# Halved background products, another DMA queue and centred projection weights in a fused attention and feed-forward kernel

## The chip, the cores and the metric

The kernel runs on one core of a Trainium2 chip. The core has a matrix engine (PE, TensorE, with its weight loads shown apart as PEld), three engines for elementwise work and reductions (DVE = VectorE, ACT = ScalarE, POOL = GpSimd), a synchronisation engine (SP) that mostly issues DMAs, and DMA queues that SP, ACT and POOL can each feed. Every engine works through its own instructions in order and waits for others through semaphores. The metric is the device time of one execution in microseconds (us), given as the median of several runs. A profile is a further execution, recorded by the hardware, with its own time.

## The reference

One transformer-like layer over a sequence of 4096 tokens with 256 features, all in float32: causal attention with 16 heads of 16 features, and a feed-forward part with four ternary weight matrices and 1024 hidden features. Cut to what matters:

```python
def _L0_attn_ref(x, w_attn, b_attn, w_proj, b_proj):
    q, k, v = jnp.split(x @ w_attn + b_attn, 3, axis=-1)      # then split in 16 heads
    logits = jnp.einsum('bhqd,bhkd->bhqk', q, k) * scale
    weights = jax.nn.softmax(jnp.where(causal, logits, -jnp.inf), axis=-1)
    out = jnp.einsum('bhqk,bhkd->bhqd', weights, v)
    return out @ w_proj + b_proj
...
x = x + _layernorm(_L0_attn_ref(_layernorm(x), ...))
x = x + _layernorm(_L0_ffn_ref(_layernorm(x), ...))
```

Two facts are used below: the layer norm of the attention's output follows the projection `w_proj` directly, and a layer norm subtracts the mean over the 256 features of each token.

## The kernel before

**Blocks and items.** The sequence is cut into NB = 8 blocks of QB = 512 tokens, block j being four tiles of 128 tokens (NT = 4). Attention works block by block over queries, and in a block over G = 4 groups of four heads: 32 items (j, g). An item goes over the key tiles kt = 0 to 4j + 3. `steps(j)` lists its steps: one for each key tile up to the first on the diagonal, and two that pack the three narrower diagonal tiles. A step has two units (`SharedUnit`, one in the last step), one for each pair of heads. So an item has 8j + 5 units, and attention 1056.

**A unit** is three pieces of work. `products()` (line 843) multiplies q and k on PE into a two-bank tile `s` of PSUM, 128 x 1024 scores. `maximum()` (line 852) reduces these to a running maximum on DVE. `finish()` (line 859) takes the exponential of the tile on ACT, with a per-block shift that was set from earlier maxima, and on diagonal tiles POOL zeroes the masked part with `affine_select` (line 866). There are three tiles `s`, so the scores of a unit wait for the exponential three units earlier. `Values.step` (line 930) multiplies the exponentials with v into `av`, some units later.

**Order.** Everything stands under a manual schedule: each engine executes in the order in which the Python code emits. The main loop emits a unit's scores, then perhaps a values step, then its maximum and exponential, and after each step calls `bg.even(...)`, which emits pieces of background work.

**Background work** is a queue of generators. `prep(j)` makes the features of block j: it loads and normalises x (mean and spread by two ACT passes, `mean_of` and `spread_of`, or by DVE for the first two blocks), transposes it on PE (`pt`, line 633), and multiplies it with the attention weights: `features` for k and q (`pk`, `pq`, line 525) and then `pv` for v (line 650). `features` copies the product to `full` (ACT, line 534), splits it in a rounded high part `hi` (line 542) and the rest `lo` (line 544), and stores each twice in DRAM (line 549), from where `queries` and `keys` load rows for the scores (line 557). In blocks 0 and 1 the split is on DVE and the `lo` stores are issued by POOL; later the split is on POOL and all stores are issued by SP. `full`, `hi`, `lo`, for k and for q, and the bank of the products are single buffers. `project(j)` loads the attention's output, scales it by the reciprocal sums on POOL, multiplies it with `w_proj` (`py`, line 314), copies it and adds the bias, takes the mean (`mean_of`, line 203) and the squared deviation (`spread_of`, line 211) of each tile on ACT, scales and shifts by them on POOL (line 224) and adds x. `halve_weights` rounds the feed-forward weights on POOL, four operations at a time (lines 1009 to 1012), one round in four steps.

A generator yields a mark before a piece: `PE`, `ACT` or True, and `HALF` between two pieces of one accumulation, which keeps the bank to that job. `even(every)` counts steps and emits one PE piece when the count is a multiple of `every`, and one ACT piece one step before that. `every` is 1 in blocks 0 and 1, 2 in blocks 2 and 3, and 3 later; from block 2 on, it isn't called on the diagonal steps. A PE piece is one matmul with 512 columns of a `pk` or `pq` (there are two to a product), or two matmuls with 256 columns for one tile of `pv` or `py`.

**The start.** `prep(0)` and `prep(1)` are run up to their transposes, then `biases()` folds the value bias through `w_proj` into `bp` (line 1106), then `prep(0)` is run to its end, with the loads of the first two items in between. `prep(1)` is left to the background.

**After attention** the feed-forward part runs over the eight blocks with split (high and low) activations on PE; the last projection, `project(7)`, runs there.

## Time and profile before

| | |
|---|---|
| median of 3 runs | 2053.86 us (2051.06 to 2056.44) |
| the profiled execution | 2048.42 us |
| its span, first to last instruction | 2046.5 us |
| mean granted PE clock | 0.986 |
| first maximum / last maximum of attention | 39.81 / 1374.4 us |
| granted clock from 39.8 to 92.8 us (block 0) | 0.77 |

Busy time in stretches that begin with the first maximum of a block, in us:

| stretch | length | units | PE | DVE | ACT | POOL |
|---|---|---|---|---|---|---|
| start | 39.8 | | 16.3 | 11.0 | 6.4 | 17.1 |
| block 0 | 53.0 | 20 | 39.9 | 29.0 | 30.0 | 17.0 |
| block 1 | 75.1 | 52 | 68.0 | 63.5 | 66.8 | 37.4 |
| block 2 | 107.0 | 84 | 97.4 | 99.7 | 102.1 | 53.9 |
| block 3 | 147.9 | 116 | 135.4 | 137.7 | 136.9 | 68.4 |
| block 4 | 185.7 | 148 | 161.6 | 173.5 | 174.1 | 79.4 |
| block 5 | 216.7 | 180 | 186.3 | 209.8 | 206.0 | 91.8 |
| block 6 | 253.8 | 212 | 218.7 | 246.2 | 240.9 | 95.0 |
| block 7 | 295.4 | 244 | 245.0 | 288.1 | 275.4 | 38.0 |
| feed-forward | 672.1 | | 656.8 | 351.4 | 160.7 | 54.2 |

A line of the groups reads: line of the code, engine, operation, tile written <- tiles read, shape written <- shape read, count | busy time, mean ns of one | idle time of the engine just before them, and what ended most of it. A line of the timeline reads: start, length (both in us), engine, line, operation, tiles, shapes, count of instructions merged, and in brackets the idle time before and what ended it. The length of merged instructions runs from the start of the first to the end of the last. Instructions of one engine overlap a little, so the time from start to start is shorter than the mean time of one.

### The profile page before, as it was taken

To read this page: it belongs to the slowest core of one execution; us is meant where nothing else is said; L and a number is where in the kernel's file an instruction comes from. 1 tells how busy PE (TensorE), PEld (TensorE's weight loads), DVE (VectorE), ACT (ScalarE), POOL (GpSimd) and SP (SyncE) were. 2 spreads that over 40 slices of the span, in tenths; PEclk is the share of its full clock that TensorE was granted. 3 is DMA by queue.
4 is the path that set the end of the run, shared out by engine and by line. 5 is a ranking of instruction groups with operands and counts; after the bars stand their busy time and mean duration, and the time that the engine had idled before them with its cause. 6 is when DMAs were issued, how large, how long until landed. Compare 5 with 4: busy or idle time off the path is not lost.

```text
span 2046.5 us, 28401 instructions
## 1 busy us (share of the span) xinstructions
PE 1825.3 (89%) x10518; PEld 932.5 (46%) x10518; DVE 1609.8 (79%) x1894; ACT 1399.2 (68%) x1598; POOL 552.2 (27%) x871
## 2 busy tenths in 40 slices
PE   4799989988888888888888887889999999999997
PEld 2333332322322322223222222228888888888886
DVE  3689998998999999999999999985546456465453
ACT  2699999999999999999999998982212222222221
POOL 3264545434435335333333110000120000000000
PEclk8899999999999999999999998999999999999999
DMA  6756645444235333553234213103100000000000
GB/s 168 229 179 219 191 133 180 147 154 159 98 131 183 116 103 124 161 163 115 76 136 156 98 44 101 63 9 114 53 11 21 15 7 21 1 21 21 1 11 15
DMA packets 134909, 202.09 MB, mean 99 GB/s; under 512 B 16064, under 2 KB 60736, under 8 KB 134752
## 3 DMA queue, kind: packets, MB, share of 16 engines
q1 hardware_dynamic: 130496, 194.56, 29.3%
q0 software_dynamic: 2480, 4.35, 1.0%
q8 instruction: 87, 1.43, 0.3%
q10 hardware_dynamic: 1776, 1.18, 0.3%
q14 instruction: 70, 0.57, 0.1%
HBM read 137.91 MB, written 62.13 MB: 98 GB/s over the span
## 4 chain that ended last, share of the span: by engine, by line
PE 46%; ACT 21%; DVE 19%; issue 6%; DMA 4%; POOL 2%; SPq 1%; ACTq 0%; POOLq 0%; DVEq 0%
PE z L1358 21%; ACT e_s L859 19%; DVE mx L852 18%; PE av L930 7%; PE s L843 7%; PE za L1358 3%; PE zb L1358 2%; PE pyf L1440 2%; DMA k<-k 1%; PE py L314 1%; PE pk L525 1%; PE pv L650 1%; PE pq L525 1%; ACT junk L211 1%; DMA q<-hiq 0%
## 5 line engine op out<-in xcount | busy, mean ns | idle before, releaser
L852 DVE TENSOR_REDUCE mx<-s 128x1 f32<-128x1024 f32 x1056 | 1219.8, 1217 | 72.1 <-PE s L843 66.6
L859 ACT ACTIVATE e_s<-s,shift 128x1024 f32<-128x1024 f32 x1056 | 1153.6, 1117 | 104.9 <-DVE mx L852 81.9
L843 PE MATMUL s<-q,k 64*128 64x512 f32 (+3 forms) x2304 | 517.7, 468 | 161.2 <-ACT e_s L859 144.7
L930 PE MATMUL av<-e_s,v 128*32 128x512 f32 (+2 forms) x4576 | 572.8, 575 | 7.9 <-POOL e_s L866 5.7
L843 PEld LDWEIGHTS s<-q,k 64*128 64x128 f32 x2304 | 208.9, 185 | 752.9 <-ACT e_s L859 652.2
L1425 ACT ACTIVATE fb<-z,sh 128x512 f32<-128x512 f32 x128 | 88.1, 689 | 364.8 <-PE z L1358 340.2
L1358 PE MATMUL z<-hb_0l,h 128*128 128x512 f32 x512 | 199.5, 390 | 0.0
L1358 PE MATMUL z<-hb_0h,h 128*128 128x512 f32 x512 | 199.5, 390 | 0.0
L866 POOL TENSOR_SCALAR_AFFINE_SELECT e_s<-e_s 128x256 f32<-128x256 f32 (+1 forms) x224 | 94.7, 440 | 337.4 <-ACT e_s L859 337.4
L233 POOL TENSOR_TENSOR rstd<-ve,neghalf 128x4 f32<-128x4 f32 (+1 forms) x22 | 20.8, 944 | 608.8 <-DVE ve L231 603.0
L930 PEld LDWEIGHTS av<-e_s,v 128*32 128x32 f32 x4576 | 97.2, 109 | 151.5 <-issue 116.1
L1325 DVE CAST hb_1h<-fb 128x512 fp32r<-128x512 f32 x64 | 27.4, 428 | 155.7 <-ACT fb L1425 155.7
L1402 ACT ACTIVATE sl<-za,s 128x512 f32<-128x512 f32 x64 | 44.0, 690 | 120.4 <-PE za L1358 60.9
L1325 DVE CAST hb_0h<-fb 128x512 fp32r<-128x512 f32 x64 | 28.1, 440 | 99.6 <-ACT fb L1425 99.6
L1358 PEld LDWEIGHTS z<-hb_0h,h 128*128 128x128 f32 x512 | 96.1, 188 | 20.0
L1358 PEld LDWEIGHTS z<-hb_0l,h 128*128 128x128 f32 x512 | 96.2, 188 | 19.8
L1011 POOL TENSOR_SCALAR wc<-wc 128x256 f32<-128x256 f32 x88 | 75.8, 861 | 7.8
L1010 POOL TENSOR_TENSOR wc<-wc,wh 128x256 f32<-128x256 f32 x88 | 64.3, 730 | 7.2
L1012 POOL TENSOR_TENSOR fit<-fit,wc 128x256 f32<-128x256 f32 x88 | 64.2, 730 | 7.3
L1009 POOL CAST wh<-wc 128x256 fp32r<-128x256 f32 x88 | 35.0, 397 | 108.4 <-DMA wc<-in_h_t_dram 75.9
L1440 PE MATMUL pyf<-w,hb_1l 128*128 128x256 f32 x256 | 61.8, 284 | 0.0
L1440 PE MATMUL pyf<-w,hb_1h 128*128 128x256 f32 x256 | 61.7, 283 | 0.0
(257 smaller groups left out, 1970.3 us busy)
## 6 DMA issues: line engine op xcount, KB each, us to landing
k<-k SPq DMA_DIRECT2D x288, 256.0 KB
q<-q SPq DMA_DIRECT2D x64, 256.0 KB
x<-in_x_dram SPq DMA_DIRECT2D x16, 512.0 KB
k<-hik SPq DMA_DIRECT2D x32, 256.0 KB
q<-hiq SPq DMA_DIRECT2D x32, 256.0 KB
wc<-in_h_t_dram SPq DMA_DIRECT2D x64, 128.0 KB
r_h<-wh SPq DMA_DIRECT2D x64, 128.0 KB
h<-r_h SPq DMA_DIRECT2D x32, 256.0 KB
```

The source lines that it names most:

```text
L843: nc.tensor.matmul(self.both[:, i, col : col + n], lhsT=kT[G * j + g, c, pr][r, tt * P : (tt + 1) * P], rhs=qT[j, g][pr][r, QB - n :], sta ...
L852: nc.vector.tensor_reduce(next(columns), self.both.rearrange("p a n -> p (a n)"), AX.X, ALU.max)
L859: nc.scalar.activation(e, self.both, AF.Exp, bias=shifts[j])
L866: nc.gpsimd.affine_select(out=here, in_=here, compare_op=ALU.is_ge, fill=0.0, base=0, pattern=[[0, here.shape[1]], [1, P]], channel_multip ...
L930: nc.tensor.matmul(self.av[h * HW : (h + 1) * HW, QB - n :], lhsT=vb[kt // NT][:, kt % NT, o : o + HW], rhs=of(es, h), start=(kt == 0 or k ...
L1010: nc.gpsimd.tensor_tensor(w, w, hi, ALU.subtract)
L1011: nc.gpsimd.tensor_scalar(w, w, 0.0, None, ALU.is_equal)
L1012: nc.gpsimd.tensor_tensor(fit, fit, w, ALU.mult)
L1325: nc.vector.tensor_copy(hi, full)
L1358: nc.tensor.matmul(ps, lhsT=w[c], rhs=single(part[:, c, :]), start=(c == 0 and i == 0), stop=(c == kc - 1 and i == parts - 1),)
L1425: nc.scalar.activation(h, z, AF.Gelu, scale=sc[:, oc : oc + 1])
L1440: nc.tensor.matmul(ps[:, 0:D], lhsT=single(part[:, c, t * P : (t + 1) * P]), rhs=(w3_r if halves else w3_sb)[:, c, :], start=(c == 0 and i ...
```

## The change

**Halves of pieces.** In the attention pass, `pk` and `pq` are computed for 256 of the 512 tokens at a time, each over both parts of the features, so that a product has four pieces (one matmul with 256 columns each) in place of two. `pv` and `py` give a piece for each matmul, and the four transposes of a bank are split in two and two.

**Rates.** `even(products, every, acts)` emits up to `products` PE pieces when the count of steps is a multiple of `every`, and an ACT piece once in `acts` steps. Blocks 0 and 1 get two PE pieces a step, blocks 2, 3, 4 and 7 one piece a step, blocks 5 and 6 one piece in two steps. ACT pieces come every 1, 1, 2, 2, 3, 4, 4, 2 steps. Block 2 now gets pieces on its diagonal steps too.

**Queue.** The low halves of block 0 are stored through ACT's queue in place of POOL's; those of block 1 stay on POOL's.

**Ahead of the first scores** `prep(1)` is run until its first k product is stored: two banks of transposes, the product `pk`, its split and the issue of its stores.

**Centred weights.** `biases()` subtracts from each row of `w_proj` its mean over the output features, and from `bp` its mean, so that the projection's output has mean zero over the features. `project` (for all blocks but the last) drops `mean_of` and the shift: `spread_of` takes the plain square, and POOL only scales.

**Order.** Before the first block's feed-forward norm is queued, in item (7, 2), `project(6)` is run to its end.

```diff
-    def even(self, every):
+    def even(self, products, every, acts):
...
         self.at += 1
-        pe, act = not self.at % every, not (self.at + 1) % every
+        pe = 0 if self.at % every else products
+        act = self.at % acts == 1 % acts
         for job in list(self.work):
             if job[3] in (self.PE, self.HALF):
-                if pe and self.open in (None, job):
-                    pe = False
+                while pe and job[3] in (self.PE, self.HALF) and self.open in (None, job):
+                    pe -= 1
                     self.run(job)
...
             for t in range(2):
-                yield room.within(t)
                 for c in range(DC):
+                    mark = room.within(DC * t + c, c > 0)
+                    if mark:
+                        yield mark
                     nc.tensor.matmul(
...
             for t in range(NT):
-                mean_of(y[:, t, :], mv, t)
-                yield Background.ACT
-                spread_of(y[:, t, :], mv, t)
+                spread_of(y[:, t, :], mv, t, 0.0)
                 yield Background.ACT if t < NT - 1 else True
...
+                nc.gpsimd.tensor_scalar(
+                    y[:, t, :], y[:, t, :], rstd[:, t : t + 1], None, ALU.mult
+                )
...
-                def within(self, n):
-                    return Background.HALF if shared and n else Background.BESIDE
+                def within(self, n, fine=False):
+                    if shared:
+                        return Background.HALF if n else Background.BESIDE
+                    return None if fine else Background.BESIDE
...
-                for d in range(DC):
-                    yield room.within(d)
+                cuts = 2 if shared else 1
+                for n, (cut, d) in enumerate(product(range(cuts), range(DC))):
+                    yield room.within(n)
+                    at = slice(cut * QB // cuts, (cut + 1) * QB // cuts)
                     nc.tensor.matmul(
-                        ps,
+                        ps[:, at],
                         lhsT=wqk[d][:, i * D + c * P : i * D + (c + 1) * P],
-                        rhs=xTs[j][:, d, :],
+                        rhs=xTs[j][:, d, at],
...
-                        queue = nc.gpsimd if shared and j < 2 and half else nc.sync
+                        queue = (nc.scalar, nc.gpsimd)[j] if shared and j < 2 and half else nc.sync
...
                     for t in range(NT):
+                        if shared and t == NT // 2:
+                            yield Background.HALF
                         nc.tensor.transpose(
...
             def biases():
                 nc.vector.tensor_scalar(bqk[:, 0:DC], bqk[:, 0:DC], SCALE, None, ALU.mult)
+                mean = stat.tile([P, DC], F32, tag="mean", name="mean")
+                nc.vector.tensor_reduce(mean, wp, AX.X, ALU.add)
+                nc.vector.tensor_scalar(mean, mean, -1.0 / D, None, ALU.mult)
+                for c in range(DC):
+                    nc.vector.tensor_scalar(
+                        wp[:, c, :], wp[:, c, :], mean[:, c : c + 1], None, ALU.add
+                    )
...
                 nc.vector.tensor_tensor(bp, bp, ps, ALU.add)
+                nc.vector.tensor_reduce(mean[:, 0:1], bp, AX.X, ALU.add)
+                nc.vector.tensor_scalar(mean[:, 0:1], mean[:, 0:1], -1.0 / D, None, ALU.mult)
+                nc.vector.tensor_scalar(bp, bp, mean[:, 0:1], None, ALU.add)
...
                 bg.work[0][3] = Background.PE
+                while ("k", 1, 0) not in stored:
+                    bg.step()
...
+                    bg.finish(("project", NB - 2))
                     bg.add(("norm", 0), norm_block(0, room, first_features), NORM)
...
-                    if j < 2 or p < NT * j:
-                        bg.even(1 + j // 2 - j // 6)
+                    if j < 3 or p < NT * j:
+                        bg.even(1 + (j < 2), 1 + (4 < j < NB - 1), (1, 1, 2, 2, 3, 4, 4, 2)[j])
```

More of the change, by code (lines that the diff above doesn't have):

```diff
@@ L2 @@
 from contextlib import ExitStack
-from itertools import chain, cycle
+from itertools import chain, cycle, product
 import concourse.bass as bass
@@ L205, in mean_of, with spread_of @@
         )
-    def spread_of(src, mv, t):
+    def spread_of(src, mv, t, shift=None):
         lent.append(True)
@@ L211, in spread_of @@
         nc.scalar.activation(
-            junk, src, AF.Square, bias=mv[:, t, 0:1], accum_out=mv[:, t, 1:2]
+            junk,
+            src,
+            AF.Square,
+            bias=mv[:, t, 0:1] if shift is None else shift,
+            accum_out=mv[:, t, 1:2],
         )
@@ L347, in project @@
         for t in range(NT):
-            (normalize if last else shift_and_scale)(
-                y[:, t, :], y[:, t, :], mv, rstd, t, nc.gpsimd
-            )
+            if last:
+                normalize(y[:, t, :], y[:, t, :], mv, rstd, t, nc.gpsimd)
+            else:
+                nc.gpsimd.tensor_scalar(
+                    y[:, t, :], y[:, t, :], rstd[:, t : t + 1], None, ALU.mult
+                )
             nc.gpsimd.tensor_tensor(y[:, t, :], y[:, t, :], xj[:, t, :], ALU.add)
@@ L647, in prep @@
                     for t in range(2):
-                        yield room.within(t)
                         for c in range(DC):
+                            mark = room.within(DC * t + c, c > 0)
+                            if mark:
+                                yield mark
                             nc.tensor.matmul(
@@ L1269, in feed_forward, with within @@
             class Room:
-                def within(self, n):
-                    return Background.BESIDE
+                def within(self, n, fine=False):
+                    return None if fine else Background.BESIDE
                 def bank(self, name):
```

## The prediction, made before the changed kernel was run

> **What bounds the kernel now.** I read the shares of busy time, the groups by line, stretches by block, then the timeline where the largest engine pauses.
>
> ```profile
> PE 1825.3 (89%) x10518; PEld 932.5 (46%) x10518; DVE 1609.8 (79%) x1894; ACT 1399.2 (68%) x1598; POOL 552.2 (27%) x871
> ...
> L852 DVE TENSOR_REDUCE mx<-s 128x1 f32<-128x1024 f32 x1056 | 1219.8, 1217 | 72.1 <-PE s L843 66.6
> L859 ACT ACTIVATE e_s<-s,shift 128x1024 f32<-128x1024 f32 x1056 | 1153.6, 1117 | 104.9 <-DVE mx L852 81.9
> ```
>
> Attention runs from the first maximum (39.81 us) to the last (1374.4), the feed-forward part from there to 2046.5. The second is the tensor engine's (656.8 busy of 672.1) and keeps its instructions, so it counts as unchanged. In attention, 1056 units pass through scores (PE), maximum (DVE), exponential (ACT), with three score tiles. Five maxima back to back take 5.75 us, one alone 1.23: the pace is (5.75 - 1.23)/4 = 1.13 us. 1056 x 1.13 = 1193 us of the stretch's 1334.6; the other 141 us are DVE's small work and its waits. ACT can do an exponential in 1.0 us (a small activation starts 1.0 after it), so it has about 12% to spare. What the waits are:
>
> ```profile
> 649.02 0.51 PE L843 MATMUL s<-q,k 64*128 64x512 f32 x2
> ...
> 649.46 1.13 PE L525 MATMUL pq<-xT,wqk 128*128 128x512 f32 x2
> ...
> 650.51 0.49 PE L843 MATMUL s<-q,k 64*128 64x512 f32 x2
> ...
> 650.94 1.07 PE L930 MATMUL av<-e_s,v 128*32 128x512 f32 x8
> 651.05 1.23 DVE L852 TENSOR_REDUCE mx<-s 128x1 f32<-128x1024 f32 x1 [0.19 <-PE s L843]
> ...
> 651.93 0.73 PE L843 MATMUL s<-q,k 64*128 64x512 f32 x4
> ...
> 652.47 1.22 DVE L852 TENSOR_REDUCE mx<-s 128x1 f32<-128x1024 f32 x1 [0.19 <-PE s L843]
> ```
>
> The background product `pq` occupies PE for 1.05 us (649.46 to the next scores at 650.51). The following scores are late, the maximum starts 0.28 us over the pace; the scores after it stand behind `av` and are again 0.29 late. One such product costs 0.57 us. In blocks 4 to 7 this pair returns every 7.36 us, where three steps of 2.26 us should take 6.79.
>
> **Products in halves of what they were.** The program order of the old kernel has 85 such products among the scores of blocks 2 to 7 (15, 19, 17, 14, 16, 4). In blocks 4 to 7: 51 x 0.57 = 29 us. In blocks 2 and 3 the rows show less, 0.3 to 0.65; with 0.45, 34 x 0.45 = 15. Together 44 us.
>
> The new order has 169 pieces of half the length (34, 31, 32, 34, 30, 8), never more than one before a unit except once at block 2's start. The nearest row is `pv`: four passes of 256 columns take 1.06 us (656.81 to 657.87) against 1.05 for two of 512. So a piece is 0.53. A step without a product costs PE 0.99 (`av`) + 0.67 (651.93 to 652.59, two units of scores) = 1.66 us; with a piece 0.43 + 0.53 + 0.44 + 0.99 = 2.39 against 2.26: a piece in every step loses 0.13 us, on and on. That is so in blocks 2, 3, 4 and 7: 105 x 0.13 = 14 us. Blocks 5 and 6 have one in two steps; two steps then cost 4.05 of 4.52, the first delay (0.53 + 0.19 of switching) lies under the 0.96 that the old product had free (1.24 - 0.28), and the 0.30 behind `av` leaves 0 to 0.06: 64 x 0.06 = 4 at most, I take 3. Gain 44 - 17 = **27 us**. Bounds: 0.25 a piece at full rate (ACT's insertions come on top) gives 15; no loss in blocks 5 and 6 and 0.08 elsewhere gives 36.
>
> The Trainium skill ("TensorE: Matmul & The Clock Gate", Back-to-back issue gap) speaks against this: in streams of weight load and matmul it gives 81 ns for 128 columns and 131 for 512, so halving the columns saves far less than half. As an estimate from that page, 98/131 for 256 columns, a piece would be 0.79 us and a full-rate step lose 0.39; 105 x 0.39 + 64 x 0.2 = 54, and the 27 us would be a loss of 10. The `pv` row differs, and I go by the row.
>
> Block 1 keeps its rate (two pieces a step) but two old products moved out of it; a step with one is 2.91 against 2.26: 2 x 0.65 = **1 us**.
>
> **Centred weights.** Seven blocks lose four `Identity` passes each: 28 x 0.40 us of ACT (the next exponential starts 0.306 + 0.093 later) = 11 us of work. Upper bound 11; lower 0, as ACT has room and DVE only rarely waits for them alone (0.38 at the start of some items, beside the copy of `av`). Nearer the lower: **2 us**. GpSimd's scale with one operation instead of two (0.55 us) counts nothing: it is 27% busy.
>
> It costs at the start. The order makes the bias product wait for `wp` minus its mean.
>
> ```profile
> 12.37 2.05 PE L1106 MATMUL pb<-wp,bv 128*128 128x256 f32 x4 [12.37 <-DMA wp<-in_w_proj_dram]
> ...
> 13.07 0.16 DVE L1103 TENSOR_SCALAR bqk<-bqk 128x2 f32<-128x2 f32 x1
> ...
> 14.21 1.06 PE L633 MATMUL pt<-ident,x 128*128 128x128 f32 x4
> ```
>
> DVE is free at 13.23; a reduction of 512 columns took 0.68 (L922), a tiny scaling 0.16, two passes of 256 columns 0.32 + 0.41 (L237): 1.57, so the product starts at 14.9 instead of 12.37, and all behind it on PE (transposes, features of block 0) 2.5 us later: **-2.5 us** to the first scores. The three operations on `bp` fit before DVE's next work at 20.02 + 2.5.
>
> **The start: queue and early products.** The low halves' issue leaves GpSimd (0.60 us each) for ScalarE. Behind a waiting issue on ScalarE stand `fullq`, the next `fullk` and the copies of `v`, and the products wait for these because their bank is single.
>
> ```profile
> 30.21 0.69 DVE L544 TENSOR_TENSOR lok<-fullk,hik 128x512 fp32r<-128x512 f32 x1 [3.65 <-DMA k<-lok]
> 33.75 0.43 DVE L542 CAST hiq<-fullq 128x512 fp32r<-128x512 f32 x1 [2.85 <-ACT v L658]
> ...
> 39.81 1.23 DVE L852 TENSOR_REDUCE mx<-s 128x1 f32<-128x1024 f32 x1 [4.90 <-PE s L843]
> ...
> 50.70 2.08 PE L525 MATMUL pk<-xT,wqk 128*128 128x512 f32 x2
> ...
> 53.54 1.23 DVE L852 TENSOR_REDUCE mx<-s 128x1 f32<-128x1024 f32 x1 [3.37 <-PE s L843]
> ```
>
> The second `lok` waits for the first low store to land (issued at 22.2, landed 30.1). Stores on SP's queue land about 4.8 us after issue, so by that row the second `lok` stays near 30 despite the 2.5, but its two issues then hold ScalarE to about 31.5, and `loq` to about 36. The copies of `v`, block 1's transposes and first `pk` (0.7, 0.6, 0.7, 0.6, 2.0) follow: first scores near 43.5 instead of 38.98. Besides, in the new order block 1's first `hik` stands on DVE ahead of the first maximum and overwrites a tile whose stores SP issues behind eight loads; in the old run these landed at 45.5 and 46.8. So the first maximum comes at 45 to 48: 5 to 8 us late, the 2.5 among them.
>
> Against it: the stalls for block 1's transposes (1.0 at 48.95) and first `pk` (3.46 at 53.54, over the pace) are gone, one of three feature stalls of 2.9 to 3.3 us moves ahead, and block 1's stores leave an item earlier, so the DMA waits before items (0,3) and (1,0) (6.2 and 4.0 us over the pace at 80.28 and 92.84) shrink by 0 to 8. Sum: -6.5 + 1.0 + 3.5 + 2.9 + 2 = **3 us** earlier at 92.84; bounds -5 and +9.
>
> "DMA: Bandwidth & Descriptors" (Rules for kernel authors) says that spreading transfers over issuing engines saves issue time alone, since all use the same 16 DMA engines. The row says more (7.9 against 4.8 us to land, though under different load); by the rule the second `lok` comes 2 to 3 us later and the start gains nothing.
>
> **POOL at the ends of items.** The masks of an item's last units queue behind background work on GpSimd, and `av` waits.
>
> ```profile
> 346.00 0.72 POOL L1012 TENSOR_TENSOR fit<-fit,wc 128x256 f32<-128x256 f32 x1
> 346.68 2.79 POOL L866 TENSOR_SCALAR_AFFINE_SELECT e_s<-e_s 128x256 f32<-128x256 f32 x7
> 347.15 2.28 PE L930 MATMUL av<-e_s,v 128*32 128x512 f32 x8 [1.82 <-POOL e_s L866]
> ...
> 350.20 1.22 DVE L852 TENSOR_REDUCE mx<-s 128x1 f32<-128x1024 f32 x1 [3.23 <-PE s L843]
> ```
>
> Four items of the old run lose 1.65, 3.32, 3.16 and 0.85 us so, 9 in all, each with 4.6 to 9.4 us of GpSimd work issued in the last six units. The new order puts such a pile before the ends of items (4,2) (7.5 us), (3,0) and (2,1): about 3.3 + 1 + 0.7, and 1 for another. **3 us** gained; bounds -4 and +8.
>
> **Sum.** 27 + 1 + 2 + 3 + 3 = 36 us, of which I take 34, as the pieces at full rate have no slack left for anything else. The profiled execution was 2048.4 (span 2046.5), below all three runs (2051.1 to 2056.4, median 2053.9); from the median, 2053.9 - 34 = **2020 us**.
>
> **Rivals.**
> - *Full rate is too fast.* With a piece in each step and no slack, ACT's 0.4 to 0.7 us insertions add in blocks 2 to 4: 0.28 a piece instead of 0.13 takes 15 us back, and the gain is 19: 2035. For it: losses of 0.35 instead of 0.28 where ACT inserts. Against: ACT's own pace (1.0) gives 0.13 a unit back. Chance 0.24.
> - *The start is dear.* The first maximum at 48 and block 1's loads no earlier: -5 instead of +3: 2028. Chance 0.12.
> - *The switch costs, not the length* (the other side). If a piece costs the 0.29 behind `av` whatever its length, 169 x 0.29 = 49 us against 44; with the start at -5 and POOL at -4 the time is 2053.9 + 5 + 5 + 4 - 3 = 2065. It decides from 0.26 us a piece (44/169). For it: half of today's loss is that second 0.29. Against: it followed a first delay that used up the slack. Chance 0.08.
> - *The means were the bound after all*: 11 instead of 2 gives 2011. Chance 0.12.
>
> **How the numbers follow.** Main case 0.44 at 2020. Range 2002 to 2043: products at 36 with the means at 8 below, products at 15 with the start at -5 above; about 0.2 lies outside. A change under 0.3% (6 us) can't be told from none here. Faster 0.86 (all but the switch rival and tails), same 0.06, slower 0.08.
>
> **What would show it.** In blocks 5 and 6, maxima back to back through the products and stretches of 1.15 us a unit (1.20 to 1.24 now); in blocks 2 to 4 steps of about 2.39 us. First maximum at 45 to 48 us, item (1,0) before 92. `Identity` rows of `y` absent. Wrong, if each piece in blocks 5 and 6 still has its pair of late maxima, or if block 1 begins after 95.

## The result, and the profile after

The changed kernel took 2072.91 us (median of 4 runs, 2072.26 to 2076.05), the old one beside it 2052.46 (2049.47 to 2056.44). The ratio is 1.0105, 95% interval 1.0089 to 1.0121: slower by 1%, some 20 us, where 34 us faster were forecast. The time lies outside the range and beyond every rival.

The page of the changed kernel, shares of busy time and the two costliest groups (the last columns are idle time before the group and what ended it):

```profile
PE 1855.8 (90%) x10646; PEld 952.9 (46%) x10646; DVE 1610.8 (78%) x1901; ACT 1394.2 (67%) x1542; POOL 559.0 (27%) x863
...
L868 DVE TENSOR_REDUCE mx<-s 128x1 f32<-128x1024 f32 x1056 | 1219.7, 1216 | 80.3 <-PE s L859 68.0
L875 ACT ACTIVATE e_s<-s,shift 128x1024 f32<-128x1024 f32 x1056 | 1157.0, 1117 | 105.8 <-DVE mx L868 86.1
```

The work is the same, cut into 128 more instructions on PE; PE is busy 30 us longer, and the maxima wait 80.3 us instead of 72.1. The two profiled executions lie 24.5 us apart (spans of 2071.0 and 2046.5), the medians 20.5. Where the span grew, from the first maximum of each stretch to that of the next, in us:

| stretch | before | after | difference |
|---|---|---|---|
| up to the first maximum | 39.8 | 54.2 | +14.4 |
| block 0 | 53.0 | 50.1 | -2.9 |
| block 1 | 75.1 | 76.0 | +0.9 |
| block 2 | 107.0 | 126.9 | +19.9 |
| of it item (2,1) | 26.1 | 41.1 | +15.0 |
| blocks 3, 4 | 333.5 | 336.5 | +3.0 |
| blocks 5, 6 | 470.5 | 460.8 | -9.7 |
| block 7 | 295.4 | 294.5 | -0.9 |
| feed-forward | 672.1 | 672.0 | -0.1 |

So only blocks 5 and 6 did what was forecast. Three places lost: the start (+11.4 at item (1,0)), one item of block 2, and the steps of blocks 2 to 4 that should have gained 12 us and did not.

**The quarters.** A quarter is one of the four pieces of a product, one matmul over 256 columns (two instructions in the profile); "full rate" is one in each step. Timeline of the changed kernel, PE and DVE, first in block 4 (a quarter in each step), then in block 5 (one in two steps):

```profile
479.44 0.51 PE L859 MATMUL s<-q,k 64*128 64x512 f32 x2
...
481.15 0.70 PE L537 MATMUL pq<-xT,wqk 128*128 128x256 f32 x2 [1.20 <-ACT fullk L546]
...
482.32 1.23 DVE L868 TENSOR_REDUCE mx<-s 128x1 f32<-128x1024 f32 x1 [0.75 <-PE s L859]
...
483.64 0.70 PE L537 MATMUL pq<-xT,wqk 128*128 128x256 f32 x2
484.27 0.50 PE L859 MATMUL s<-q,k 64*128 64x512 f32 x2
484.69 1.07 PE L946 MATMUL av<-e_s,v 128*32 128x512 f32 x8
485.69 0.50 PE L859 MATMUL s<-q,k 64*128 64x512 f32 x2
486.11 0.70 PE L537 MATMUL pq<-xT,wqk 128*128 128x256 f32 x2
...
661.24 35.76 DVE L868 TENSOR_REDUCE mx<-s 128x1 f32<-128x1024 f32 x31
...
666.64 0.70 PE L537 MATMUL pk<-xT,wqk 128*128 128x256 f32 x2
667.27 0.49 PE L859 MATMUL s<-q,k 64*128 64x512 f32 x2
667.69 1.06 PE L946 MATMUL av<-e_s,v 128*32 128x512 f32 x8
668.69 1.12 PE L859 MATMUL s<-q,k 64*128 64x512 f32 x4
```

In block 5, 31 maxima run back to back at 1.15 us through the products (661.24): the old pair of late maxima is gone. But a quarter holds PE from 483.64 to 484.27, 0.63 us, not the 0.53 that was read off `pv`, and a full-rate step lasts 486.11 - 483.64 = 2.47 against 2.26: it loses 0.21, not 0.13. At 481.15 a quarter stood in PE's queue 1.20 us for `fullk`, which frees the single bank and waits its turn among the exponentials: with an insertion of ScalarE near it, a quarter at full rate lost 0.46 to 0.53 us on the mean of a block (e7, under "Why the prediction was wrong").

**The start.** Timeline of the changed kernel, ScalarE's and its queue's rows, and what stands behind them on PE and DVE:

```profile
25.15 2.15 ACTq L561 DMA_DIRECT2D k<-lok  x2
27.36 0.69 ACT L546 ACTIVATE fullq<-pq,bqk 128x512 f32<-128x512 f32 x1 [3.42 <-DMA k<-lok]
29.26 1.95 ACTq L561 DMA_DIRECT2D q<-loq  x2
...
38.57 0.43 DVE L554 CAST hiq<-fullq 128x512 fp32r<-128x512 f32 x1 [4.99 <-DMA q<-hiq]
39.75 1.20 ACTq L561 DMA_DIRECT2D q<-loq  x2
41.00 0.59 ACT L674 COPY v<-pv 128x512 f32<-128x512 f32 x1 [4.51 <-DMA q<-loq]
...
46.99 3.66 PE L537 MATMUL pk<-xT,wqk 128*128 128x256 f32 x8 [0.67 <-ACT xT L651]
50.58 0.73 PE L859 MATMUL s<-q,k 64*128 64x512 f32 x4
...
53.10 0.43 DVE L554 CAST hik<-fullk 128x512 fp32r<-128x512 f32 x1 [13.38 <-DMA k<-hik]
...
54.17 1.22 DVE L868 TENSOR_REDUCE mx<-s 128x1 f32<-128x1024 f32 x1
```

Each of the first three pairs of stores holds ScalarE for 1.95 to 2.15 us. The last pair waits until `loq` exists at 39.7: `hiq` ahead of it came 2.1 us after its `fullq` (done at 36.49), as it waited for the store of the `hiq` before. So the first copy of `v` comes at 41.00 (30.46 before), and the transposes, the early products (the first takes 3.66 us, where the prediction had 2.0) and the first scores after it. Then `hik` waits on DVE for stores that SP issued behind eight loads.

**Item (2,1).** Two stalls of 4.5 and 4.9 us. Timeline of the changed kernel, GpSimd, PE, SP's queue and ScalarE:

```profile
208.40 0.19 POOL L223 TENSOR_SCALAR ve<-mvy 128x4 f32<-128x4 f32 x1
208.68 1.04 POOL L225 TENSOR_TENSOR rstd<-ve,neghalf 128x4 f32<-128x4 f32 x1
209.82 0.93 POOL L356 TENSOR_SCALAR y<-y,rstd 128x256 f32<-128x256 f32 x1
210.84 0.73 POOL L359 TENSOR_TENSOR y<-y,x 128x256 f32<-128x256 f32 x1
211.52 0.60 POOL L554 CAST hik<-fullk 128x512 fp32r<-128x512 f32 x1
212.20 1.26 POOL L556 TENSOR_TENSOR lok<-fullk,hik 128x512 fp32r<-128x512 f32 x1
213.42 1.26 POOL L308 TENSOR_TENSOR oo<-oo,xT0lo 128x512 f32<-128x512 f32 x1
214.64 0.65 POOL L882 TENSOR_SCALAR_AFFINE_SELECT e_s<-e_s 128x512 f32<-128x512 f32 x1
215.34 1.08 PE L946 MATMUL av<-e_s,v 128*32 128x256 f32 x8 [3.81 <-POOL e_s L882]
...
218.94 1.93 PE L946 MATMUL av<-e_s,v 128*32 128x512 f32 x8
...
222.97 0.37 SPq L361 DMA_DIRECT2D x<-y  x1
225.19 1.19 SPq L561 DMA_DIRECT2D q<-hiq  x2
226.81 1.53 SPq L561 DMA_DIRECT2D q<-loq  x2
228.39 0.73 SPq L165 DMA_DIRECT2D x<-in_x_dram  x1
...
236.88 0.42 ACT L204 ACTIVATE junk<-x 128x256 f32<-128x256 f32 x1 [4.83 <-DMA x<-in_x_dram]
```

First a mask stands behind 6.2 us of background work on GpSimd (208.40 to 214.64) and `av` behind the mask. Then ScalarE's first pass over block 4's `x` waits 4.83 us for a load that SP issued only at 228.39, behind the store of `y` and the stores of `q`; the exponentials stand behind it. After each stall PE runs at half pace for a few passes (`av` 1.93 against 1.07 us).

### The profile page after: what moved, and what is told of

It is laid out like the page before. It is cut to its first block, busy times and chain, and to the rows that moved or that the text cites. A ratio compares the mean times of both kernels' runs of the same rounds, so it can differ in the third digit from the quotient of the medians.

```text
span 2071.0 us, 28657 instructions
## 1 busy us (share of the span) xinstructions
PE 1855.8 (90%) x10646; PEld 952.9 (46%) x10646; DVE 1610.8 (78%) x1901; ACT 1394.2 (67%) x1542; POOL 559.0 (27%) x863
## 4 chain that ended last, share of the span: by engine, by line
PE 46%; DVE 22%; ACT 19%; DMA 5%; issue 4%; POOL 2%; SPq 1%; ACTq 0%; POOLq 0%; DVEq 0%
PE z L1387 22%; DVE mx L868 20%; ACT e_s L875 17%; PE av L946 6%; PE s L859 5%; PE za L1387 3%; PE zb L1387 3%; PE pyf L1469 3%; DMA k<-k 1%; PE py L321 1%; DMA x<-in_x_dram 1%; PE pv L666 1%; DMA invd<-sums 1%; PE pq L537 1%; DMA k<-lok 1%
## 5 line engine op out<-in xcount | busy, mean ns | idle before, releaser
L868 DVE TENSOR_REDUCE mx<-s 128x1 f32<-128x1024 f32 x1056 | 1219.7, 1216 | 80.3 <-PE s L859 68.0
L859 PE MATMUL s<-q,k 64*128 64x512 f32 (+3 forms) x2304 | 527.5, 471 | 124.5 <-ACT e_s L875 110.0
L882 POOL TENSOR_SCALAR_AFFINE_SELECT e_s<-e_s 128x256 f32<-128x256 f32 (+1 forms) x224 | 94.8, 441 | 417.9 <-ACT e_s L875 417.9
L1387 PEld LDWEIGHTS z<-hb_0h,h 128*128 128x128 f32 x512 | 96.1, 188 | 19.9
L1387 PEld LDWEIGHTS z<-hb_0l,h 128*128 128x128 f32 x512 | 96.1, 188 | 19.9
```

Source lines behind the costliest of these rows:

```text
L859: nc.tensor.matmul(self.both[:, i, col : col + n], lhsT=kT[G * j + g, c, pr][r, tt * P : (tt + 1) * P], rhs=qT[j, g][pr][r, QB - n :], sta ...
L868: nc.vector.tensor_reduce(next(columns), self.both.rearrange("p a n -> p (a n)"), AX.X, ALU.max)
L882: nc.gpsimd.affine_select(out=here, in_=here, compare_op=ALU.is_ge, fill=0.0, base=0, pattern=[[0, here.shape[1]], [1, P]], channel_multip ...
L1387: nc.tensor.matmul(ps, lhsT=w[c], rhs=single(part[:, c, :]), start=(c == 0 and i == 0), stop=(c == kc - 1 and i == parts - 1),)
```

## The experiments

All start from the changed kernel unless "old kernel" is said. The times are medians, with the ratio to the old kernel run on the same chip and its 95% interval.

**e1, e2: the start, one part undone at a time.**

```
e1: -queue = (nc.scalar, nc.gpsimd)[j] if shared and j < 2 and half else nc.sync
    +queue = nc.gpsimd if shared and j < 2 and half else nc.sync
e2: -while ("k", 1, 0) not in stored:
    -    bg.step()
```

> Block 0's low halves go back to GpSimd's queue, the rest of the change stays. Theory (ScalarE's queue is the start's main cost: its issues of 1.9 to 2.2 us a pair and their waits stand ahead of fullq, fullk and the copies of v): the first copy of v leaves ScalarE near 34 us instead of 41.0, the first maximum falls at about 48 instead of 54.2, item (1,0) begins near 99 instead of 104.3, and the whole takes 5 to 7 us less than the changed kernel, about 2067. Rival (the early products and the wait of hik for its own stores set the first maximum): the first maximum stays above 52 and the whole within 2 us of 2073.

> The four products ahead of the first scores are dropped, the queue stays ScalarE's. Theory (they cost what they take on PE, 44.4 to 50.6, plus the wait of block 1's first hik, and give the old feature stalls back): first maximum at about 45.5 instead of 54.2, item (1,0) 2 to 5 us earlier than 104.3, the whole about 2069. Rival (they are only moved: what the first maximum gains, the items of block 0 lose): first maximum near 45.5 too, but item (1,0) within 1 us of 104.3 and the whole within 2 us of 2073.

e1: 2075.74, ratio 1.0117 (1.0098 to 1.0136). The start went the theory's way (copy of `v` at 32.5, first maximum at 50.7, item (1,0) at 97.7; of these 6.6 us at (1,0) some 4 are the pace of PE in the two executions, see g1 to g3), and the whole gained nothing: block 2 took 129.0 and block 4 190.7 (126.9 and 185.8). e2: 2061.61, ratio 1.0046 (1.0029 to 1.0063), first maximum at 46.9, item (1,0) at 99.2, 5 us earlier; 11 us less in all, so more than its theory, because item (2,1) fell to 33.6 as well.

**e3: weights of the projection not centred.** (Undoes the diff's parts in `spread_of`, `project` and `biases`.)

> Weights of the projection as they were: no mean is taken from wp and bp, and ScalarE's 28 Identity passes and GpSimd's scale with two operations come back. Theory (centring is worth next to nothing in the steps and costs 1.7 us at the start and 0.37 us of GpSimd in each of 28 scales): pb at 12.4, first scores about 1.7 us earlier, the stall of 4.5 us near 217 shorter by 1 to 2 us, the whole between 2068 and 2074. Rival (the Identity passes were a real bound, 28 x 0.40 us): 5 to 11 us slower than the changed kernel, 2078 to 2084.

2060.63, ratio 1.0039 (1.0023 to 1.0056): 12 us faster than the changed kernel, below both expectations. `pb` comes at 12.2, but most of it is item (2,1): 29.9 us instead of 41.1. With four more passes of ScalarE per projection the scales of `y` come later and are no longer in the pile before the mask. In blocks 5 to 7 next to nothing moved (755.0 in all, against 755.3), so the passes cost nothing there.

**e4: more steps between a load and its first use.**

```
-for _ in range(2):
+for _ in range(2 if j < 4 else 6):
     yield True
 yield Background.ACT
```

> From block 4's preparation on, ScalarE's first pass over x is issued four steps later after the load (six steps instead of two); nothing else. Theory (the stall of 4.9 us at 239 is this pass standing in ScalarE's queue for a late load, and the clock that falls during it costs another 2 us): item (2,1) falls from 41.1 to 34 us, the whole to about 2066. Rival (the wait only moves, because the products that follow are then late): item (2,1) shorter, but block 2 with its four items still above 124 us (126.9 now), the whole within 2 us of 2073.

2058.22, ratio 1.0031 (1.0018 to 1.0043). The pass over `x` in e4's timeline, with no wait in brackets:

```profile
239.56 0.41 ACT L204 ACTIVATE junk<-x 128x256 f32<-128x256 f32 x1
```

Item (2,1) fell to 34.5 and block 2 to 118.2, as the theory had it; the stall at GpSimd (4.5 us) stayed. The whole gained 15 us where 7 were expected; block 3 was 2.3 and block 4 1.9 us shorter too. So this wait is shown as the cause of the second stall.

**e5: the scale on GpSimd with two operations.**

```
-y[:, t, :], y[:, t, :], rstd[:, t : t + 1], None, ALU.mult
+y[:, t, :], y[:, t, :], zero[:, t : t + 1], rstd[:, t : t + 1], ALU.add, ALU.mult
```

> GpSimd's scale of y gets its second operation back (a zero is added first), so that it takes 0.55 us instead of 0.93; the order of all else stays that of the changed kernel. Theory (the stall of 4.5 us at 217 in item (2,1) is the mask standing behind this pile on GpSimd): the pile ahead of the mask is 0.4 to 0.8 us shorter, the stall 3.5 to 4, and as the tensor engine idles less the slow passes behind it go too; item (2,1) 36 to 40 instead of 41.1, the whole 2 to 5 us below 2073. Rival (that the uncentred kernel lost this stall was the work falling elsewhere, not the length of the scale): stall and whole as before, within 2 us.

```profile
209.77 0.56 POOL L358 TENSOR_SCALAR y<-y,zero,rstd 128x256 f32<-128x256 f32 x1
...
214.21 0.65 POOL L884 TENSOR_SCALAR_AFFINE_SELECT e_s<-e_s 128x512 f32<-128x512 f32 x1
```

e5's timeline, GpSimd: the scale takes 0.56 instead of 0.93, and the stall 3.38 instead of 4.48 us (3.5 to 4 expected); item (2,1) 39.7. The whole, 2071.13 (ratio 1.0094, 1.0077 to 1.0111), can't be told from the changed kernel, as the rival had it. The pile's place weighs more than the length of this one operation (e3 against e5).

**e6: half rate in block 2.**

```
-bg.even(1 + (j < 2), 1 + (4 < j < NB - 1), (1, 1, 2, 2, 3, 4, 4, 2)[j])
+bg.even(1 + (j < 2), 1 + (j in (2, 5, 6)), (1, 1, 2, 2, 3, 4, 4, 2)[j])
```

> In block 2 the quarters come in one step of two, as in blocks 5 and 6, instead of in each; blocks 3 and 4 stay at one a step and take over what is left. Theory (full rate leaves no slack, so that each insertion of ScalarE or a late mask stays as loss): block 2 falls from 126.9 to 112 to 118 us, block 3 rises by at most 3, the whole 2060 to 2066. Rival (the two stalls of item (2,1) are a matter of where single operations fall): block 2's items (2,0), (2,2) and (2,3) lose 1 us each at most, a stall of over 3 us shows in another item, the whole within 4 us of 2073.

2068.32, ratio 1.0087 (1.0071 to 1.0104). Block 2 fell to 109.6, even below the expected 112, and items (2,0) and (2,1) to 25.8 and 25.6. But blocks 3 and 4 rose to 155.1 and 191.2 (150.7 and 185.8), with stalls of 5.2, 3.5 and 6.2 us before units of (2,3), (3,0) and (4,1) that had 2.0 us or less before. Both theories are half right: the rate was most of block 2's loss, and more than half of what it gave back (17.2 us) went into blocks 3 and 4 (9.8). The profiled execution, at 2060.20, was the fastest of four; the median gained 4.6 us.

**e7: the quarters alone.** (e1, e2 and e3 together. The rates of the changed kernel stay, ACT's too, and so do the halved transposes, the pieces on block 2's diagonal steps and the order of `project(6)`: no run takes these apart from the quarters.)

> Only the quarters with their rates are kept: block 0's low halves on GpSimd's queue, no products ahead of the first scores, weights of the projection not centred. Theory (start and item (2,1) hold all of the loss, the quarters gain in blocks 5 and 6 what they lose in block 2): item (1,0) begins at 92 to 94, block 2 at 113 to 119, blocks 5 and 6 together 9 to 11 us under the old kernel's, the whole 2048 to 2056, no difference from the old kernel that can be told. Rival (the quarters gain 27 us as predicted and the rest hid it): 2030 or less. Rival (the quarters are the loss): above 2060.

2053.40, ratio 1.0007 (0.9995 to 1.0018), as the theory had it. Item (1,0) begins at 92.7. Against the old kernel blocks 2, 3 and 4 are 8.0, 1.0 and 4.0 us longer, blocks 5, 6 and 7 are 4.4, 5.9 and 1.2 shorter: the quarters with their rates are worth nothing as they stand.

**e8, e9, e12: what seemed best, put together.** e8: low halves on GpSimd's queue, no early products, e5's scale, e4's steps, one quarter in two steps in blocks 3 to 6. e9 and e12 go on from it:

```
e9:  -if j < 3 or p < NT * j:
     +if j < 3 or p < NT * j - 2 * (j > 2):
     -if j > 0 and p % 4 == 2 and p < NT * j:
     +if j > 0 and p % 4 == 0 and p < NT * j:
e12: as e9, and
     -1 + (2 < j < NB - 1)
     +1 + (j in (2, 4, 5, 6) and p < NT * j)
```

> What the runs so far favour, together: low halves on GpSimd's queue, no early products, the scale with two operations, six steps between load and first pass of x from block 4's preparation on, one quarter in two steps in blocks 3 to 6; weights stay centred. If the losses are separate: item (1,0) begins near 94.5 (centring 1.7), block 2 near 115, blocks 3 and 4 each 3 us under the old kernel's like blocks 5 and 6, so about 2036 to 2045. If a stall only moves to another item whenever work is shifted: 2050 or more.

> The mix (e8), with GpSimd kept clear before an item's masks: background work stops two steps before the diagonal in blocks 3 to 7, and the weight halving steps come at the steps 0, 4, 8 of an item instead of 2, 6, 10. Theory (what the mix gains in blocks 3 to 6 it gives back in masks that stand behind GpSimd's background work: stalls of 2.5, 8.0, 1.3, 2.6 and 2.0 us at the second units of items): these stalls go, 12 to 16 us, the whole about 2038 and faster than both kernels. Rival (the background work that is pushed out of the ends piles up in the middle and stalls there): stalls of over 2 us at other places, the whole 2048 or more.

> The mix with clear ends, but with one quarter in two steps in block 2 (on its diagonal one a step) and in blocks 4 to 6, and one a step in block 3. Theory (a quarter costs 0.3 us or more at full rate and 0.1 to 0.2 at half rate): block 2 falls to 107 to 111 from 111.7 in the mix, block 3 rises by 5 from 143.9, the whole equal to the mix with clear ends within 4 us. Rival (block 2's delay comes from the late masks and loads, not from the rate): block 2 not under 111, block 3 up by 5, the whole 5 us slower.

e8: 2051.82, ratio 1.0004 (0.9994 to 1.0013), the case in which stalls move. Block 3 did fall to 143.9, and item (4,1) paid with a stall of 8.0 us at its start. e8's timeline, GpSimd and PE:

```profile
465.62 1.28 POOL L310 TENSOR_TENSOR oo<-oo,xT0lo 128x512 f32<-128x512 f32 x1 [15.88 <-DMA xT0lo<-invd]
469.85 1.26 POOL L310 TENSOR_TENSOR oo<-oo,xT0lo 128x512 f32<-128x512 f32 x1 [2.96 <-DMA xT0lo<-invd]
...
475.19 2.79 POOL L884 TENSOR_SCALAR_AFFINE_SELECT e_s<-e_s 128x256 f32<-128x256 f32 x7
475.65 2.28 PE L948 MATMUL av<-e_s,v 128*32 128x512 f32 x8 [6.34 <-POOL e_s L884]
```

GpSimd's queue stands at a product that waits for its DMA (2.96 us idle), and seven masks come out late in a row. e9: 2052.66, ratio 1.0003 (0.9992 to 1.0014): a miss, this stall was 8.9 us (the product that waits for its DMA is issued ahead of the steps that were kept clear). e12: 2046.91, ratio 0.9964 (0.9950 to 0.9978), better than e9 by more than expected: block 2 at 108.9, block 4 at 181.1 without the stall. Block 3, back at full rate, took 149.6 where e9 took 142.5 at half rate.

**e10: e9 with uncentred weights; e11: the old kernel with e9's two edits alone.**

> The same with the projection's weights not centred, so with 28 Identity passes on ScalarE again. Theory (the passes cost nothing in the steps, blocks 5 to 7 differed by less than 2 us in all between the kernels with and without them): starts 2 us earlier and ends within 4 us of the centred one. Rival (once the stalls are gone the passes are the next bound): 5 to 11 us slower than the centred one.

> The old kernel with the same two edits for its ends and nothing of the change. Theory (its own stalls of this kind, 1.65, 3.32, 3.16 us at 275, 350 and 472, go too): 2043 to 2047. So if the mix with clear ends gets 2038, some 5 to 9 us of that are the quarters'. Rival (the ends are all there is to gain): within 3 us of the mix with clear ends.

e10: 2060.83, ratio 1.0038 (1.0024 to 1.0052), 8 us over e9. That is the rival's size but not all its mechanism: blocks 5 and 6 are 1.5 and 1.9 longer, block 7 8.6, with one stall of 4.8 us where ScalarE's copy of `y` waited for the store of the projection before. e11: 2043.34, ratio 0.9954 (0.9941 to 0.9967): the old kernel's own stalls at 350 and 472 are gone, that at 275 is not, and it is faster than both kernels.

**g1, g2, g3: queue, centring and early product, each alone in the old kernel.** (The diff's lines for each; the early product is one uncut `pk`, that is two products in halves.)

> The old kernel with block 0's low halves on ScalarE's queue and nothing else of the change. Theory (each pair of issues holds ScalarE for 1.9 to 2.2 us ahead of the next full and v): first maximum at 46 to 49 instead of 39.8, item (1,0) 4 to 7 us later than 92.8, blocks 1 to 7 as before, the whole 2056 to 2060. Rival (as predicted: the earlier landing pays for the issues): item (1,0) within 1.5 us of 92.8, the whole within 2 us of the old kernel.

> The old kernel with the projection's weights centred and nothing else. Theory (1.7 to 2.5 us at the start, nothing gained by the missing Identity passes in the steps): first maximum 41.5 to 44, item (1,0) at 94.5 to 96, blocks 5 to 7 in sum within 2 us of the old kernel's, the whole 2052 to 2057. Rival (the means were a bound): blocks 2 to 7 in sum 6 us shorter or more, the whole 2048 or less.

> The old kernel with block 1's first product ahead of the first scores. Theory (the product delays the first scores by the transposes and itself, and its hik stands ahead of the first maximum until block 0's stores have landed; what was stalled later is given back only in part): first maximum at 45 to 50, item (1,0) 1 to 4 us later than 92.8, the whole 2054 to 2058. Rival (only moved): first maximum as late, item (1,0) within 1 us of 92.8 or earlier, the whole within 2 us of the old kernel.

g1: 2053.16, ratio 1.0003 (0.9993 to 1.0014); g3: 2051.99, ratio 1.0001 (0.9989 to 1.0013); g2: 2048.51, ratio 0.9980 (0.9968 to 0.9993). Alone, queue and early product cost nothing that can be told in the whole, and centring gains about 4 us. All three begin item (1,0) late (99.2, 95.9, 97.2 against 92.8), but a part of that is not theirs. The starts of two kernels with the same work there, e7 and h2, PE:

```profile
17.32 1.99 PE L536 MATMUL pk<-xT,wqk 128*128 128x256 f32 x8 [0.68 <-ACT xT L650]
```

```profile
17.69 3.78 PE L541 MATMUL pk<-xT,wqk 128*128 128x512 f32 x4 [0.67 <-ACT xT L655]
```

In some executions the first products take 3.5 to 3.8 us instead of 2.0: the first one alone, or the first two or three. It was so in 11 of the 20 profiled ones, the changed kernel's among them (one slow product), the old kernel's not. Sorted by that, with the number of slow products in brackets, the begin of item (1,0), in us (h1 and h2, whose means are taken behind the bias product, count as none):

| parts of the change at the start | `pk` 2.0 us | `pk` 3.5 to 3.8 us |
|---|---|---|
| none | 92.7, 92.8, 93.8, 93.9 | 94.8 (1), 97.1 (2), 98.7 (3) |
| centring | 95.2, 95.9 | 98.5 (2), 100.0 (3) |
| queue | | 99.2 (1) |
| early product(s) | | 97.2 (1) |
| centring, early | 97.7 | |
| centring, queue | | 99.2 (1) |
| early, queue | | 102.6 (1) |
| all | 99.2, 100.6 | 104.3 (1), 104.0 (2) |

Each slow product costs some 2 us, so only equal numbers of them can be compared (the mean of the first column without any part is 93.3). All parts together then cost 6.6 us with no slow product, 9.5 with one and 6.9 with two. Centring costs 1.3 to 2.3 (nothing beside the queue alone), the queue 2.2 to 5.4, the early products 2.1 to 5.1, most where the queue is changed too. What is left of the 11.4 us between the two profiles, 2 to 5, is the pace of PE in that execution. Single executions carry this table, and its differences of 2 us rest on one or two each.

**g4, h1, h2: is there a form in which the quarters pay?** g4: e12 with uncentred weights and the scale as it was. h1: e11 with centred weights and e5's scale, the mean of `wp` taken off behind the bias product (the mean of `bp` is taken off after it, so the result is the same). h2: h1 with quarters for the preparations of blocks 6 and 7 and the projections of blocks 3 to 6 only, one piece in two steps in blocks 4 to 6 and one a step in block 7; ACT's rates and the order of `project(6)` are the changed kernel's.

> Quarters at half rate in blocks 2 and 4 to 6 and at full rate in block 3, clear ends, the old start, weights not centred. To be set against the old kernel with clear ends (2043.3). Theory (a quarter costs 0.1 us at half rate and 0.3 at full rate, an old product about 0.43): blocks 2 to 7 gain 36 - 30 = 6 or more over the old kernel, less what forced products cost at the ends of block 4 (about 4), so 2040 to 2046, equal to the old kernel with clear ends within 4 us. Rival (at half rate the quarters bring what was predicted of them): 2030 or less.

> The old kernel with clear ends and centred weights, the centring placed behind the bias product (the mean taken from bp after the product makes up for the uncentred wp in it), so that the product waits for nothing new; GpSimd's scale keeps two operations. If the two gains add (old kernel with clear ends 2043.3, centring 3.7 of 2052.2, 2 to 3 at the start now spared): 2037 to 2041. If centring gained only by where it put other work: 2043 to 2047.

> The same, with quarters for the preparations of blocks 6 and 7 and for the projections of blocks 3 to 6, that is in blocks 4 to 6 at one in two steps and in block 7 at one a step; halves before that. Theory (quarters gain where they leave slack: blocks 4 to 6 were 2.2, 3.4 and 2.6 us shorter with them than in the old kernel with clear ends): blocks 1 to 3 equal to h1 within 3 us, blocks 4 to 6 together 6 to 9 us shorter, the whole 4 to 9 us below h1, 2030 to 2037. Rival (the quarters' gain is eaten by forced products and by late work in block 7): within 3 us of h1 or slower.

g4: 2053.27, ratio 1.0012 (1.0000 to 1.0023), above both expectations. Blocks 4, 5 and 6 are 2.3, 3.5 and 2.6 us shorter than e11's, block 3 at full rate 8.2 longer, block 2 1.8, block 7 5.0 (the wait of the copy of `y` again). h1: 2044.20, ratio 0.9959 (0.9946 to 0.9973): centring adds nothing to e11. h2: 2042.47, ratio 0.9946 (0.9932 to 0.9959). Blocks 5 and 6 are 6.2 and 3.3 shorter than h1's, block 4 is 8.5 longer (a load of `x` waited for on ScalarE, 2.9 us, and late masks, 4.2). e11, h1 and h2 all beat both kernels by some 9 us against the old one and can't be told apart.

## Why the prediction was wrong

**The sum.** It can be put together from the runs: 7 to 9 us at the start (the table), 12 in the stalls of item (2,1) (41.1 against 29.1 in e7), 1.6 from the quarters (e7). That is 21 to 23, and 20.5 were measured. The closeness proves little: the first two terms come from single profiles, and the parts don't add (e2, e3 and e4 each undid one thing and gained 11, 12 and 15 us).

**Products in halves: +27 forecast, -2 measured.** The mechanism was right at half rate: blocks 5 and 6 gained 9.7 us, where the prediction's own numbers (30 old products by 0.57, less 3) make 14. The term was mis-sized in two places. The piece: "So a piece is 0.53" took the half of four `pv` passes, but two passes of the feature product hold PE for 0.63. And the insertions of ScalarE, which find no slack at full rate. In e7, over the two maxima around each quarter and without those that hold other DVE work, 117 quarters of blocks 2 to 4 lost 49.7 us over 2.26 each. Half of them lost 0.22 or less, as the row above; the mean is 0.42, not 0.13 (0.13 with nothing but exponentials on ScalarE near it, 0.49 with an insertion). That is the mechanism of the rival "full rate is too fast", at more than its 0.28. The old products, counted alike, lost 0.41 us in blocks 2 and 3 and 0.52 later (0.45 and 0.57 were taken), so a quarter at full rate cost as much as the old product of twice its work. Quarters at half rate, in blocks 5 and 6, lost 0.11. So blocks 2 to 4, which by the prediction's numbers should have gained 12 us, took 13 more in e7, and blocks 5 to 7 took 11.5 less. The runs with other rates bear this out: block 2 took 115.0 at full rate without the two stalls (e7) and 108.9 at half rate (g4), and between e9 and e12, which differ in rates alone, block 3 took 7.1 us more at full rate.

The estimate from the Trainium skill ("TensorE: Matmul & The Clock Gate", Back-to-back issue gap) had been 0.79 us for a piece and a loss of 10 us for the whole term. The row is 0.63, between that and the prediction's 0.53; half the columns do cost more than half the time here, as the page has it. The whole term, at -2, came out nearer to that loss than to the gain of 27.

**The start: +3 forecast, -7 to -9 measured.** The failed step is "the second `lok` stays near 30 despite the 2.5, but its two issues then hold ScalarE to about 31.5, and `loq` to about 36". In the changed kernel's profile the second `lok` came at 32.9, its issues held ScalarE to 35.7, `loq` held it to 40.9, and first scores came at 50.6, not 43.5. Of this the pace of PE has a part. In e4 and e6, which have the same start and no slow product, the second `lok` did come near 30 (30.8 and 30.6). But its pair of issues took 2.3 us, where two GpSimd issues of 0.6 had been the measure, and held ScalarE to 33.8 and 33.6. Then `hiq` ahead of `loq` stood 1.6 us after its `fullq` for the store of the `hiq` before, a wait that the sum didn't have, and `loq` held ScalarE to 39.1 and 38.9. Behind that, the early `pk` took 3.5 and 3.8 us in place of 2.0, and first scores came at 48.6 and 50.1. e6's timeline, DVE, ScalarE's queue and PE:

```profile
30.60 0.69 DVE L556 TENSOR_TENSOR lok<-fullk,hik 128x512 fp32r<-128x512 f32 x1 [0.48 <-DMA k<-lok]
31.32 2.26 ACTq L561 DMA_DIRECT2D k<-lok  x2
...
35.93 0.43 DVE L554 CAST hiq<-fullq 128x512 fp32r<-128x512 f32 x1 [4.64 <-DMA q<-hiq]
...
46.42 3.78 PE L537 MATMUL pk<-xT,wqk 128*128 128x256 f32 x8 [0.68 <-ACT xT L651]
```

So the price of a pair of issues on ScalarE was too low, and the wait for the store of `hiq` was missing. The wait of `hik` was foreseen, at 45 to 48 instead of 53. Of the stalls to be given back (7.4 us in three terms) block 0 gave 3. The rival "the start is dear" had the right place and 5 of the 7 to 9 us. "Wrong, if block 1 begins after 95" was met: at 104.3, and in the three other profiles with this start at 99.2 to 104.0.

**Centred weights: the start's 2.5 was about right** (1.3 to 2.3 by the table, `pb` 1.7 later). In the steps the passes are worth nothing by e3; alone (g2) the centred old kernel gained 4 us, but on top of clear ends (h1) nothing, so that gain looks like a matter of where the work fell. With quarters and clear ends, though, leaving out the centring made block 7 8.6 us (e10 against e9) and 7.0 us longer (g4 against e12). What the passes are worth thus stays open. Counting the scale on GpSimd at nothing was wrong in itself: it grew from 0.55 to 0.93.

**POOL at the ends of items: +3 forecast, -4.5 in one place.** The pile before the end ahead of (2,1) was named and priced at 0.7; with 6.2 us of it ahead of one mask it cost 4.5. What no term held is the second stall: a load issued later on SP, waited for on ScalarE. The prediction asked what stands behind a waiting instruction for the start alone, not for the passes over `x`.

## What to carry to other kernels

A filler that leaves no slack in a step turns every insertion of another engine into loss; give it a rate at which two steps together still have room, and measure its size on its own row, not on a longer one divided. In a kernel with in-order queues, each background instruction that may wait (a load on ScalarE, a DMA on GpSimd, a single buffer) must be issued late enough that it never does, for the critical work stands behind it. When one edit shifts all that follows, its own worth shows only with the shifted stalls taken off stretch by stretch; here clearing the ends of items, two lines, gained 10 us where the whole change lost 20.

## What the runs showed of the hardware that was not expected

- GpSimd's scale of 128x256 by one operand and one operation took 0.93 us (28 of 28, 0.91 to 0.94), by two operands and two operations 0.55 (0.56 in e5).
- Two stores issued by ScalarE one after the other held it 1.95 to 2.15 us in the changed kernel (1.20 once), 1.2 to 2.4 in the six other kernels with that queue; on GpSimd's queue an issue took 0.60 to 0.72.
- The same first products took 2.0 us in 9 executions; in 11 others one to three of them took 3.5 to 3.8, on one chip both ways. The trace's own records of the granted clock go with this. The first record, of full clock, begins at 15.4 to 18.1 us in the 9, ahead of `pk`, and at 20.7 to 32.0 in the 11, where the pace doubles (23.1 in the changed kernel, between `pk` of 3.78 us at 19.43 and `pq` of 1.99 at 23.99). Ahead of the first record the view of the clock by stretches prints 1.00, as from 19 to 23 us in the changed kernel, while PE goes at half pace. What sets the time of that record isn't shown: PE's first product of all starts at 12.2 to 14.7 us in both groups.
- After the stall of 4.5 us in item (2,1), where `av` takes 1.93 instead of 1.07, the granted clock is 0.50 from 215 to 219 us.
